# Second scores in the common PSUM banks for the first group, and gate/up products placed by half blocks for the second, in a cross-attention + soft-MoE kernel

## Chip, core and metric

One core of a Trainium2 chip. The time is the device time of one execution in microseconds; three runs of the kernel before gave 1177.79 to 1178.29, median 1177.96. Everything is float32. A profiled execution is one run with the hardware profiler on.

## What is computed

`x` is 16 sequences of 100 tokens by 256, `ctx` 16 contexts of 361 by 256. Cut to what matters:

```python
x = x + xattn(layernorm(x), ctx)      # 16 heads of 16: q@k.T/4, softmax over 361 keys, @v, @wo
x = x + ffn(layernorm(x))             # soft mixture of 16 experts with 64 slots each:
#   logits  = ln(x) @ slot_embeds.T             [tokens, 1024 slots]
#   slots   = softmax over experts(logits).T @ ln(x)
#   eout    = (gelu(slots@Wg + bg) * (slots@Wu + bu)) @ Wd + bd      per expert
#   out     = softmax over slots(logits) @ eout
```

## The kernel before

The batch is cut into groups of 2, 2, 4, 4, 4 sequences (`GROUPS`, L51). For each group there are three kinds of work: the **attention units** (`units`, L862), the **dispatch** of tokens to slots (`dispatch_quarter`, L927), and the **experts** (`experts`, L1264, with `down` L1231 and `combine_quarter` L1152). The experts of group g run while the attention of group g+1 is made, so only the first group's attention (the first 80 us or so) has no expert products beside it.

**A unit** is four heads of one sequence (`Unit`, L769), one per 32-row strip of the TensorE array, numbered here 0 to 7 in the first group (four for each of two sequences). Its steps:

- `maxima` (L781): first scores, four matmuls of 361 columns (L785) into the four banks of the fixed tile `at`; a VectorE reduction over them (L790) makes the row maxima.
- `queries` (L796): TensorE transposes the maxima (L799) into spare columns of `at` bank 0, VectorE adds them to the query (L801, tile `q`), which makes the second scores come out with the maximum subtracted.
- `exponentials` (L805): second scores, three blocks of keys by four strips, twelve matmuls of 100 columns (L810), into the same four banks of `at`; one ScalarE exponential over all of them (L818, `aT`).
- `values` (L824): twelve matmuls (L833) into a tile `cx` of the common pool; ScalarE copies it to `cxs` (L842).

Because first and second scores use the same `at`, a unit's first scores wait for the exponential of the unit before (`free_t`).

**PSUM** has eight banks: four for `at`, four for the common pool `ps_mm` (`mm_tile`, L169), which every other product takes in turn.

**Order.** Each engine runs its instructions in the order in which the program issued them. That order is made at build time by a planner: each stream of work is a Python generator that yields when it can go on (`when`), how many banks it needs and what it will use of TensorE, VectorE and ScalarE (`needs`); a model clock (`Clock`, L64) books a duration for every step. The loop at L1354 takes the first task that the model finds ready; in the first group the units lead, and other work (`fill`) is put between if it fits before the next step of the units. Where nothing fits, **warm products** are issued (`warm_up`, L1339: a matmul of the identity into bank 3 of `at`, which nothing reads). Fill work of the first group:

- `key_work` (L570) for sequences 0 to 3: transposed context `c_t` (L584), keys `k_ps` (L613) copied out by VectorE (L634) and ScalarE (L639), values `v_ps` (L673); a DMA by the SP queue writes the mask row into the keys (L653).
- `query_work` (L491), `out_work` (L701: reciprocal of the softmax sums, L713 and L714, a GpSimd multiply, `o_ps`, layernorm statistics, `xn_t`), `bo_work` (L413), `parameter_work` (L397).
- `slot_work` (L451): the layernorm of the slot embeddings: statistics on VectorE (L436, L437), scaling on ScalarE (L467), `se_t` (L476) and `seT` (L482).

In `experts`, the gate (`gp`) and up (`up`) products of one block (L1284, 8 matmuls of 128 columns in groups of two sequences) are issued without a break; the planner may put other work only between blocks.

Of the kernel before, what the change touches and what calls it, by code (L numbers as in the profile page):

```python
# [47 lines left out]
P = 128  # L48
# [7 lines left out]
SLACK = 0.6  # L56
BACKLOG = 2.5
ASIDE = ("out_work", "query_work", "key_work")
MASK_DMA = 5.0
COLD = 7.0  # L60
HOP = 0.12
# [68 lines left out]
def xattn_ffn_kernel(  # L130
# [38 lines left out]
    def mm_tile(name):  # L169
        return ps_mm.tile([P, 512], F32, tag="mm", name=name)  # L170
# [320 lines left out]
    def query_work(b, n=2):  # L491

        g = group_of[b]
        i0 = b - starts[g]
        yield x_t[g], 0, (0.0, 0.65 * n, 0.0)
        mv4 = two.tile([N, 2, 2], F32, tag="mv4", name="mv4")
        for i in range(n):
            ck.run("DVE", stats(accs[g][:, i0 + i, :], N, mv4[:, i, :]), x_t[g])
        r4 = rstd(mv4[:, :n, 1], N, n)
        t = ck.run("POOL", 0.7, ck.run("DVE", 0.15))  # L500
        yield t, 0, (0.0, 0.45 * n, 0.0)
        z4 = const.tile([N, 2, D], F32, tag="z4", name="z4")
# [12 lines left out]
        xT = const.tile([P, KD, 2 * N], F32, tag="xT", name="xT")  # L515
        ps = mm_tile("x_t")
        for kd in range(KD):
            for i in range(n):
                nc.tensor.transpose(
                    ps[:, (n * kd + i) * N : (n * kd + i + 1) * N],  # L520
                    z4[:, i, kd * P : (kd + 1) * P],
                    ident[:N, :N],
                )
# [12 lines left out]
        for oc in range(KD):  # L536
            for kd in range(KD):
                nc.tensor.matmul(  # L538
                    ps[:, oc * n * N : (oc + 1) * n * N],
                    lhsT=w_sb["wq"][:, kd, oc * P : (oc + 1) * P],  # L540
                    rhs=xT[:, kd, : n * N],
                    start=kd == 0,
                    stop=kd == KD - 1,
                )
        t = max(ck.pe(400 * n, t, ck.bank()), par_t[0] if par_t[0] < NEVER else 10.5)
        for oc in range(KD):
            src = ps[:, oc * n * N : (oc + 1) * n * N]
            nc.vector.tensor_scalar(
                qp[:, oc, 0, cols], src, hm[:, 0:1], qb[:, oc, 0:1], ALU.mult, ALU.add
            )  # L550
            nc.scalar.activation(
                qp[:, oc, 1, cols], src, AF.Identity, bias=qb[:, oc, 1:2], scale=hm[:, 1:2]
            )
            first = ck.psum_dve(100 * n, t)
            t = ck.copy(100 * n, first)
            if b == oc == 0:
                qps[b] = (qp, first)
        ck.free(t)
        for i in range(n):
            qps.setdefault(b + i, (qp, t))  # L560
        yield (lambda: bo_t[0]), 0, (0.0, 0.0, 0.0)
        a = accs[g][:, i0 : i0 + n, :]
        nc.gpsimd.tensor_tensor(a, a, bo_bc[:N].unsqueeze(1).to_broadcast([N, n, D]), ALU.add)
        t = ck.run("POOL", 0.55 * n)
        for i in range(n):
            with_bo[b + i] = t
# [202 lines left out]
    class Unit:  # L769
# [35 lines left out]
        def exponentials(self):  # L805
# [15 lines left out]
            if self.cb == 3:  # L821
                live.discard(self.b)

        def values(self):  # L824
            if self.cb == 0:
                live_cxs.add(self.b)
                cxs_of[self.b] = two.tile([P, 2, KD, N], F32, tag="cxs", name="cxs")
                fill.append(Task(out_work(self.b), ck, 2))
            cx = mm_tile("cx")
            for c in range(3):  # L830
                n = KC if c < 2 else S2 - 2 * KC
                for r in range(4):
                    nc.tensor.matmul(  # L833
                        cx[32 * r : 32 * r + 32, :N],
                        lhsT=values_of[self.b][
                            :n, c, 4 * self.oc + r, 2 * self.par : 2 * self.par + 2, :
                        ].rearrange("p k w -> p (k w)"),
                        rhs=self.aT[:n, r, c * N : (c + 1) * N],
                        start=c == 0,
                        stop=c == 2,  # L840
                    )
            nc.scalar.copy(cxs_of[self.b][:, self.par, self.oc, :], cx[:, :N])  # L842
            t = ck.copy(100, ck.run("PE", 0.72, self.t, values_t[self.b], ck.bank()))
            ck.free(t)
            cx_t[self.b, self.cb] = t

    free_t = [0.0]
    phase = [""]
    cx_t = {}
    group_of = {b: g for g, n in enumerate(GROUPS) for b in range(starts[g], starts[g] + n)}  # L850
# [6 lines left out]
    def values_ready(u):  # L857
        if u.b not in values_t or (u.cb == 0 and len(live_cxs) == 2):
            return NEVER
        return max(u.t, values_t[u.b])  # L860

    def units(g):  # L862
        last = None

# [6 lines left out]
                fill.append(Task(key_work(u.b + 2), ck))  # L871

        group = range(starts[g], starts[g] + GROUPS[g])
        for b in group:
            for cb in range(4):
                yield (
                    lambda: max(keys[b, cb][1], qps[b][1]) if (b, cb) in keys and b in qps else NEVER
                ), 0, (0.0, 0.0, 0.0)
                yield free_t[0], 0, (0.8, 1.7, 0.0)
                u = Unit(b, cb)  # L880
                u.maxima()
                if cb == 0 and b % 2 == 1 and b + 1 in group:
# [348 lines left out]
    def down(g, e, hts):  # L1231
# [29 lines left out]
            done_t[g, q] = t  # L1261
        give_back((k, "wd"), (k + 1, "wd"))

    def experts(g):  # L1264
        n = GROUPS[g]
        T = n * S
# [2 lines left out]
        for e in range(E):  # L1269
# [3 lines left out]
            for part in range(FC // FB):  # L1273
# [3 lines left out]
                for kind in range(2):  # L1277
                    yield (lambda: NEVER if slots_left[g, q] else slot_t[g, q]), 1
                    load_weights()
                    w = weights[k, ("wg", "wu")[kind]]  # L1280
                    ps = mm_tile(("gp", "up")[kind])
                    for f, fc in enumerate(fcs):
                        for kd in range(KD):
                            nc.tensor.matmul(  # L1284
                                ps[:, f * T : (f + 1) * T],
# [2 lines left out]
                                start=kd == 0,  # L1288
                                stop=kd == KD - 1,
                            )  # L1290
                    t = ck.pe(1024, slot_t[g, q], ck.bank())
                    for f, fc in enumerate(fcs):
                        cols = slice(f * T, (f + 1) * T)
                        if kind == 0:
# [59 lines left out]
    while streams["experts"]:  # L1354
# [29 lines left out]
        if waiting:  # L1384
            units_first = dispatches[:WINDOW] + units_first
            side = sorted(fill, key=lambda t: t.kind != "out_work")
            if group == 1 and 0 in qps:
                kinds = (
                    "early_work",
                    "bo_work",  # L1390
                    "query_work",
                    "parameter_work",
                    "slot_work",
                    "out_work",
                    "key_work",
                )
# [18 lines left out]
        if not begun:  # L1415
# [7 lines left out]
            else:  # L1423
                lead = [
                    i
                    for i, t in enumerate(tasks)
                    if t.kind in ("out_work", "all_experts") or t in dispatches[:1]
                ] if group > 1 else []
            soonest = min((ready[i] for i in lead), default=NEVER)
            by_keys = any(t.kind in ("key_work", "later_keys") and r <= now for t, r in zip(tasks, ready))  # L1430
            for i, t in enumerate(tasks):
# [6 lines left out]
                late = 0.15 + SLACK * pe  # L1438
                if not first_units:
                    fits = max(end, vector, scalar) <= soonest + late  # L1440
                elif phase[0] == "max":
                    fits = max(end, vector) <= soonest + late and scalar <= soonest + late + 1.2
                elif phase[0] != "queries":
# [10 lines left out]
            if ready[-1] <= now:  # L1454
                ready[:-1] = [NEVER] * (len(ready) - 1)
        first = next((i for i, r in enumerate(ready) if r <= now), None)
        if first is None:
            first = min(range(len(ready)), key=lambda i: ready[i])
            assert ready[first] < NEVER
            if not begun and now + 0.2 < ready[first] and phase[0] != "queries":  # L1460
                warm_up()
                continue
        task = tasks[first]
        begun = begun or task is streams["experts"]
        task.step()
        if task.done:
# [63 lines left out]
```

## Time and profile before

| | |
|---|---|
| median of three runs | 1177.96 us |
| profiled execution | 1179.8 us |
| its span | 1178.0 us |
| TensorE clock granted | 1.00 in every slice |
| VectorE, ScalarE, GpSimd busy | 632.8, 539.8, 150.9 us |
| warm products (L1337) | 53 matmuls, of which 9 before the first real product |

The page's first part gives each engine's busy time as a share of the span; its second part cuts the span into 40 slices of 29 us and gives the busy tenths of each. "Idle before" stands ahead of an instruction, with what released it. In float32 every matmul leaves two records in the trace (a transpose leaves one), so a row "x24" is twelve matmuls.

### The profile page before, as it was taken

What the parts mean: (1) busy time and instruction counts of PE and PEld (TensorE: products, weight loads), DVE (VectorE), ACT (ScalarE), POOL (GpSimd) and SP (SyncE); (2) the same over time, 40 slices, a digit from 0 to 9 for tenths busy, and PEclk for the clock granted to TensorE, in tenths of its full rate; (3) what the DMA queues carried; (4) which work ended last, traced back from release to release, by engine and by line L of the source; (5) the groups of instructions that cost most, each with busy time, mean ns of one, the idle gap of its engine ahead of it and who ended that gap; (6) DMA issues with size and microseconds to landing.
All of it is one profiled execution on the core that took longest, in us unless ns stands there. A gap on an engine that the chain in (4) does not pass through costs nothing.

```text
span 1178.0 us, 24309 instructions
## 1 busy us (share of the span) xinstructions
PE 1160.2 (98%) x9825; PEld 899.1 (76%) x9825; DVE 632.8 (54%) x1559; ACT 539.8 (46%) x1112; POOL 150.9 (13%) x255
## 2 busy tenths in 40 slices
PE   8899999999999999999999999999999999999998
PEld 6587778787787777767777776787878878777876
DVE  5755545565654565655386767656543455442222
ACT  3557554664544667434454634646312336314110
POOL 3110301013000131300010010304000003002000
PEclk9999999999999999999999999999999999999999
DMA  4412656543566603212341321333344343345431
GB/s 134 136 38 97 233 174 203 162 145 116 154 201 220 188 11 90 83 58 100 113 105 53 111 91 38 98 126 112 112 158 137 118 148 126 112 129 163 138 131 55
DMA packets 138588, 144.85 MB, mean 123 GB/s; under 512 B 45050, under 2 KB 97228, under 8 KB 138476
## 3 DMA queue, kind: packets, MB, share of 16 engines
q1 hardware_dynamic: 137258, 141.50, 38.6%
q8 instruction: 78, 1.28, 0.4%
q0 software_dynamic: 496, 1.12, 0.3%
q10 hardware_dynamic: 722, 0.67, 0.2%
q14 instruction: 34, 0.28, 0.1%
HBM read 141.60 MB, written 1.66 MB: 122 GB/s over the span
## 4 chain that ended last, share of the span: by engine, by line
PE 94%; DVE 2%; ACT 2%; DMA 1%; issue 1%; POOL 0%; SPq 0%; ACTq 0%; DVEq 0%; POOLq 0%
PE dn L1244 19%; PE gp L1284 19%; PE up L1284 19%; PE sl L1032 5%; PE po L1162 5%; PE at L810 4%; PE at L785 4%; PE lg L942 3%; PE cx L833 3%; PE v_ps L673 3%; PE k_ps L613 3%; PE at L1337 1%; PE o_ps L726 1%; DVE mxp L790 1%; DMA w_all<-in_L_ffn_Wd_dram 1%; PE q_ps L538 1%
## 5 line engine op out<-in xcount | busy, mean ns | idle before, releaser
L1284 PE MATMUL gp<-ring,w_all 128*128 128x256 f32 (+1 forms) x1280 | 247.8, 340 | 1.3 <-ACT lg_all L963 1.3
L1284 PE MATMUL up<-ring,w_all 128*128 128x256 f32 (+1 forms) x1280 | 246.6, 340 | 0.0
L1300 DVE SCALAR_TENSOR_TENSOR hT<-up,parT,ge 128x256 f32<-128x256 f32 (+1 forms) x320 | 119.6, 423 | 233.3 <-PE up L1284 163.0
L1244 PE MATMUL dn<-w_all,hT 128*64 128x256 f32 x2048 | 232.9, 382 | 1.4 <-DMA w_all<-in_L_ffn_Wd_dram 1.3
L1295 ACT ACTIVATE ge<-gp,parT 128x256 f32<-128x256 f32 (+1 forms) x320 | 116.8, 429 | 249.5 <-PE gp L1284 245.3
L1284 PEld LDWEIGHTS gp<-ring,w_all 128*128 128x128 f32 x1280 | 203.4, 191 | 27.5 <-issue 4.9
L1284 PEld LDWEIGHTS up<-ring,w_all 128*128 128x128 f32 x1280 | 203.7, 191 | 21.4 <-issue 1.2
L1244 PEld LDWEIGHTS dn<-w_all,hT 128*64 128x64 f32 x2048 | 142.7, 137 | 79.8 <-issue 8.3
L790 DVE TENSOR_REDUCE mxp<-at 100x4 f32<-100x1444 f32 x64 | 106.2, 1660 | 30.7 <-PE at L785 30.0
L1253 DVE TENSOR_TENSOR ring<-dn,bd_bc 128x512 f32<-128x512 f32 x64 | 44.2, 691 | 136.3 <-PE dn L1244 136.2
L818 ACT ACTIVATE aT<-at 121x1200 f32<-121x1200 f32 x64 | 74.9, 1170 | 64.3 <-PE at L810 60.9
L1295 ACT ACT_TABLE_LOAD x60 | 77.0, 1283 | 26.7 <-PE gp L1284 24.3
L1012 DVE STREAM_TRANSPOSE disp<-d_ex 32x128 f32<-32x128 f32 x256 | 77.4, 302 | 4.5
L717 POOL TENSOR_TENSOR cxs<-cxs,rs 128x100 f32<-128x100 f32 x63 | 24.8, 396 | 390.7 <-DVE rs L714 363.3
L1047 ACT ACTIVATE ring<-sl,parT 128x256 f32<-128x256 f32 x64 | 32.6, 561 | 67.9 <-PE sl L1032 67.9
L1032 PE MATMUL sl<-disp,xn 100*128 100x256 f32 x256 | 63.4, 388 | 0.2 <-ACT disp L1025 0.2
L1162 PE MATMUL po<-ring,lg_all 128*100 128x256 f32 x256 | 60.5, 383 | 0.4 <-DVE ring L1253 0.2
L997 POOL TENSOR_TENSOR d_ex<-d_ex,d_sm 128x400 f32<-128x400 f32 x28 | 23.8, 852 | 267.7 <-DVE d_sm L994 240.6
L810 PEld LDWEIGHTS at<-q,kT 32*121 32x121 f32 x1344 | 40.6, 180 | 19.9 <-issue 8.8
L1032 PEld LDWEIGHTS sl<-disp,xn 100*128 100x128 f32 x256 | 46.4, 190 | 10.3 <-issue 2.6
L810 PE MATMUL at<-q,kT 32*121 32x100 f32 x1344 | 49.9, 277 | 3.4 <-DVE q L801 3.3
L818 ACT ACT_TABLE_LOAD x36 | 46.2, 1283 | 14.2 <-PE at L810 6.2
(152 smaller groups left out, 1268.4 us busy)
## 6 DMA issues: line engine op xcount, KB each, us to landing
w_all<-in_L_ffn_Wg_dram SPq DMA_DIRECT2D x80, 512.0 KB
w_all<-in_L_ffn_Wu_dram SPq DMA_DIRECT2D x80, 512.0 KB
w_all<-in_L_ffn_Wd_dram SPq DMA_DIRECT2D x80, 512.0 KB
bd_bc<-in_L_ffn_bd_dram SPq DMA_DIRECT2D x80, 64.0 KB
c_sb<-in_ctx_dram SPq DMA_DIRECT2D x96, 44.0 KB
acc<-in_x_dram SPq DMA_DIRECT2D x7, 200.0 KB
out_dram<-acc SPq DMA_DIRECT2D x7, 200.0 KB
ring<-n_L_ffn_slot_embeds_dram POOLq DMA_DIRECT2D x1, 1024.0 KB, 6.6
```

Source lines behind the costliest of these rows:

```text
L785: nc.tensor.matmul(self.at[:N, r, :S2], lhsT=self.q[rows], rhs=self.k[rows], start=True, stop=True)
L790: nc.vector.tensor_reduce(mxv[:, :, m : m + 1], self.at[:N, :, :S2], AX.X, ALU.max, negate=True)
L810: nc.tensor.matmul(self.at[: KC + 1, r, c * N : (c + 1) * N], lhsT=self.k[rows, c * KC : c * KC + KC + 1], rhs=self.q2[rows], start=True, ...
L818: nc.scalar.activation(self.aT[: KC + 1], self.at[: KC + 1, :, : 3 * N], AF.Exp)
L1012: nc.vector.transpose(dst[toks, :, :, a, :], src[32 * a : 32 * a + 32, :, :, toks])
L1032: nc.tensor.matmul(sl[:, kd * 256 : (kd + 1) * 256], lhsT=xns[g][:, b0 + i, kd * P : (kd + 1) * P], rhs=disp[:, i, :], start=True, stop=True,)
L1162: nc.tensor.matmul(pos[i][:N, :D], lhsT=lg_all[:, slot, 2 * c + i, :], rhs=eouts_of(g, q)[:, c, 2 * p + i, :], start=c == 0, stop=c == 1,)
L1244: nc.tensor.matmul(dn[S * x : S * x + S, i * D : (i + 1) * D], lhsT=hts[x][fc // FB][0].rearrange("p (f b s) -> p f b s", f=FB, s=S)[:, fc ...
L1253: nc.vector.tensor_tensor(eouts_of(g, q)[:, j // 2, 2 * half : 2 * half + 2, :], dn.rearrange("p (b d) -> p b d", d=D), biases[k // 2].uns ...
L1284: nc.tensor.matmul(ps[:, f * T : (f + 1) * T], lhsT=w[:, kd, fc * P : (fc + 1) * P], rhs=slots_of(g, q)[:, j, kd].rearrange("p b s -> p (b ...
L1295: nc.scalar.activation(ge[:, cols], ps[:, cols], AF.Gelu, bias=col(8, e, fc))
L1300: nc.vector.scalar_tensor_tensor(out=hT[:, cols], in0=ps[:, cols], scalar=col(NPAR, e, fc), in1=ge[:, cols], op0=ALU.add, op1=ALU.mult,)
```

## The change

In the first group, `first_units` takes the place of the loop in `units`. The second scores no longer go to `at`: `half_exponentials` makes them in two halves of two strips each, six matmuls and two ScalarE exponentials of 300 columns per half, in four tiles of the common pool. So the next unit's first scores may be issued before the exponentials of this unit. The order asked for is: the maxima's transpose of unit n, first scores of n+1, products `cx` of n-1, both halves of n. Around it the planner's rules change: side work of the first group is let in by a budget per unit (`spare`), a task that needs VectorE alone may go first when VectorE is about idle (`IDLE`), and the order of preference of the side work is another. For group 1 (`HALVED`), the gate and up products of a block are issued as two halves of four matmuls with a yield between them. The model's time for a query copy is also changed.

```diff
+SPARE = 0.7
+IDLE = 0.15
@@ query_work
-        t = max(ck.pe(400 * n, t, ck.bank()), par_t[0] if par_t[0] < NEVER else 10.5)
+        tm = max(ck.pe(400 * n, t, ck.bank()), par_t[0] if par_t[0] < NEVER else 10.5)
...
-            first = ck.psum_dve(100 * n, t)
-            t = ck.copy(100 * n, first)
+            first = ck.psum_dve(100 * n, tm)
+            t = max(first, ck.copy(100 * n, tm))
@@ class Unit
+        def half_exponentials(self, half):
+            if half == 0:
+                self.aT = two.tile([P, 4, 3 * N], F32, tag="aT", name="aT")
+                self.parts = []
+            ps = [mm_tile(f"sc{r}") for r in range(2)]
+            t = max(ck.bank(), ck.bank())
+            for c in range(3):
+                for r in range(2):
+                    rows = slice(32 * (2 * half + r), 32 * (2 * half + r) + 32)
+                    nc.tensor.matmul(
+                        ps[r][: KC + 1, c * N : (c + 1) * N],
+                        lhsT=self.k[rows, c * KC : c * KC + KC + 1],
+                        rhs=self.q2[rows],
+                        start=True,
+                        stop=True,
+                    )
+            tp = ck.run("PE", 0.55, self.t, t)
+            for r in range(2):
+                nc.scalar.activation(
+                    self.aT[: KC + 1, 2 * half + r], ps[r][: KC + 1, : 3 * N], AF.Exp
+                )
+                t = ck.act("exp", 290, tp)
+                ck.free(t)
...
+    def first_units(finish, group):
+        held = before = None
+        nexts = [(b, cb) for b in group for cb in range(4)] + [None, None]
...
+        for n in nexts:
+            if held:
+                yield held.t, 0, (0.15, 0.25, 0.0)
+                held.queries()
+                phase[0] = "max"
+            if n and there(n):
+                yield from scores(n)
+            if before:
+                lt = before
+                yield (lambda: values_ready(lt)), 1, (0.7, 0.0, 0.3)
+                finish(before)
+                before = None
+            if held:
+                for half in range(2):
+                    yield held.t, 2, (0.5, 0.0, 0.9)
+                    held.half_exponentials(half)
+                before = held
...
@@ units
+        if g == 0:
+            yield from first_units(finish, group)
+            return
@@ experts
+    HALVED = (1,)
...
+                    bank = ck.bank()
                     for f, fc in enumerate(fcs):
+                        if g in HALVED and 2 * f == FB:
+                            ck.pe(512, slot_t[g, q], bank)
+                            yield 0.0, 0
...
-                    t = ck.pe(1024, slot_t[g, q], ck.bank())
+                    t = ck.pe(512 if g in HALVED else 1024, slot_t[g, q], bank)
@@ main loop: order of preference of the first group's side work
+                    "key_work",
+                    "query_work",
+                    "bo_work",
+                    "parameter_work",
+                    "out_work",
+                    "slot_work",
                     "early_work",
-                    "bo_work",
-                    "query_work",
-                    "parameter_work",
-                    "slot_work",
-                    "out_work",
-                    "key_work",
...
+                elif t.kind in ("slot_work", "out_work", "bo_work", "parameter_work"):
+                    fits = ready[i] <= now and max(pe, dve, act) <= spare[0]
...
+        if not begun and ck.t["DVE"] <= now + IDLE:
+            for i, t in enumerate(tasks):
+                alone = t.needs[0] == 0 and t.needs[1] > 0
+                if alone and t.kind in ("slot_work", "out_work") and t.ready() <= now:
+                    first = i
+                    break
```

More of the change, by code (lines that the diff above doesn't have):

```diff
@@ L822, in exponentials @@
                 live.discard(self.b)
+        def half_exponentials(self, half):
[21 more added lines that the diff above has]
+                ck.free(t)
+            self.parts.append(t)
+            if half == 1:
+                self.t = t
+                if self.cb == 3:
+                    live.discard(self.b)
         def values(self):
@@ L847, in xattn_ffn_kernel @@
     free_t = [0.0]
+    spare = [0.0]
     phase = [""]
@@ L860, in values_ready, with there, scores @@
         return max(u.t, values_t[u.b])
+    def first_units(finish, group):
+        held = before = None
+        nexts = [(b, cb) for b in group for cb in range(4)] + [None, None]
+        def there(n):
+            b, cb = n
+            return (b, cb) in keys and b in qps
+        def scores(n):
+            b, cb = n
+            yield (
+                lambda: max(keys[b, cb][1], qps[b][1]) if there(n) else NEVER
+            ), 0, (0.0, 0.0, 0.0)
+            yield free_t[0], 0, (0.8, 1.7, 0.0)
+            u = Unit(b, cb)
+            u.maxima()
+            free_t[0] = u.t
+            spare[0] = SPARE
+            made.append(u)
+        made = []
+        for n in nexts:
[15 more added lines that the diff above has]
+                before = held
+            if n and not made:
+                if before:
+                    lt = before
+                    yield (lambda: values_ready(lt)), 1, (0.7, 0.0, 0.3)
+                    finish(before)
+                    before = None
+                yield from scores(n)
+            held = made.pop() if made else None
     def units(g):
@@ L1426, in xattn_ffn_kernel @@
                     for i, t in enumerate(tasks)
-                    if t.kind in ("out_work", "all_experts") or t in dispatches[:1]
+                    if t.kind in ("out_work", "slot_work", "all_experts") or t in dispatches[:1]
                 ] if group > 1 else []
@@ L1463, in xattn_ffn_kernel @@
         task = tasks[first]
+        if task.kind in ("slot_work", "out_work", "bo_work", "parameter_work"):
+            spare[0] -= max(task.needs)
         begun = begun or task is streams["experts"]
```

## The prediction

> **What bounds the kernel now.** I read the page's shares and chain first, then the stretches of time, then TensorE's timeline, because the first tells which engine is short and the last where it stands still.
>
> ```profile
> PE 1160.2 (98%) x9825; PEld 899.1 (76%) x9825; DVE 632.8 (54%) x1559; ACT 539.8 (46%) x1112; POOL 150.9 (13%) x255
> ...
> PE 94%; DVE 2%; ACT 2%; DMA 1%; issue 1%; POOL 0%; SPq 0%; ACTq 0%; DVEq 0%; POOLq 0%
> ```
>
> TensorE is busy 98% and carries 94% of the chain. So the time is a sum: TensorE's useful work, its warm products, its idle time. A change that only moves work between its stages gains nothing; it must shrink idle or warm time, or else it pays for whatever it adds to the useful work. Idle is 17.8 us (1178.0 - 1160.2): 1.37 before the first product, 3.9 after the last, 1.34 at 89-90 us, some 4.8 in scattered gaps from 230 to 605 us, and 6.3 in the first group's attention, here unit 1:
>
> ```profile
> 19.00 0.39 PE L519 MATMUL x_t<-ident,z 100*128 100x100 f32 x2
> 20.27 1.16 PE L1337 MATMUL at<-ident 128*128 128x128 f32 x8 [0.88 <-DVE mxp L790]
> 21.27 0.25 PE L799 MATMUL at<-ident,mxp 100*128 100x100 f32 x1
> 21.87 0.89 PE L810 MATMUL at<-q,kT 32*121 32x100 f32 x24 [0.35 <-DVE q L801]
> 22.69 1.14 PE L538 MATMUL q_ps<-xT,wq 128*128 128x100 f32 x8
> ```
>
> Three things are to be seen. The four warm products (x8) did not fill the wait for the maxima: they waited 0.88 us for it, since their target bank was being read, and then cost 1.0 us more. The step from transpose to second scores costs 0.6 us (21.27 to 21.87), 0.35 of it idle, in every unit. Second scores, twelve matmuls, take 0.82 us (21.87 to 22.69).
>
> VectorE sets the other half of a unit:
>
> ```profile
> 54.60 0.26 DVE L801 TENSOR_TENSOR q<-at,qp 128x100 f32<-128x100 f32 x1 [0.67 <-PE at L799]
> ...
> 54.79 0.27 DVE L713 STREAM_SHUFFLE rs<-cxs 128x100 f32<-128x100 f32 x1
> ...
> 55.09 0.78 DVE L714 RECIPROCAL rs<-rs 128x100 f32<-128x100 f32 x1
> ```
>
> A shuffle and a reciprocal hold VectorE for 1.0 us (54.79 to 55.79, where the next begins). If they stand ahead of an addition `q`, it is late by that.
>
> **The account before, up to the first gate product (82.17 us).** Start 5.6 (1.37 idle, 4.21 for nine cold warm products), idle 6.3, the other 44 warm products 10.8 (their rows, about 0.24 each), useful work 59.5.
>
> **The change part by part.**
>
> *Second scores by halves: more TensorE work.* In the trace's records the 24 passes of one unit start in six rounds of four strips: 6.6 ns between strips, 106 ns between rounds, 184 ns after the first. A round takes as long with two strips as with four, because a strip waits for its own stream. A half has six rounds of two, so both have twelve. [...] But in the rows products start in the program's order and a waiting one is not overtaken, so only the last round of one half and the first of the next overlap: eleven rounds. [...] I take 0.53, **4.2 us** over eight units, ends 0 and 5.1.
>
> *Two exponentials of 300 columns per half* in place of one of 1200 (1.17 us, L818): the nearest row is the 361-column copy (0.46 us), so 4 x 0.4 to 0.46, about 0.6 us more on ScalarE per unit. ScalarE is busy 19.7 of the 39 us from 11 to 50, so this is hidden beside TensorE; uncovered it would be 5 us.
>
> *The exponential's wait goes; what is late next?* In the changed listing (order and semaphores, no times) first scores of n+1 still wait for `q` of n. So the 0.35 does not go: the transpose is followed by first scores instead of second, again 0.66 after it (14.38 to 15.04 for unit 0), or 0.54 idle, the transpose taking 0.12 and nothing standing between. And in units 2 and 6 a shuffle and reciprocal stand ahead of `q`.
>
> *Warm products.* The listing has 53 before the first gate product, as before: no gain. Eight stand right behind unit 4's first scores, three behind its second scores, two in unit 1, one behind unit 7's first scores; all wait for a reduction. Five more behind unit 7's transpose wait for `q`, which is queued behind the slot statistics' GpSimd power (1.68 us, L447) and its user on VectorE.
>
> *Walk.* I went down the changed listing with spacings from the trace: first scores 0.80, reduction ending 2.66 after their start, `cx` 0.66, both halves 1.35, two `v_ps` 0.96, two `k_ps` 1.41, `c_t` 0.73, `q_ps` 0.95, warm 0.23 each. Unit 0 starts at 11.73 as before.
>
> - Units 1 to 3: first scores at 16.6, 20.5, 24.4 (before: 17.55, 25.00, 31.26). The pipeline works: 3.9 us per unit. Here is the part that should gain.
> - But the second sequence's keys and values are still to be made (2.8 + 2.9), with `q_ps`, `c_t` and two `cx`: unit 4 at 38.2 (before 37.66). Its reduction ends at 41.2; TensorE idles 2.2 for it, then the eight warm products take 1.85.
> - Units 5, 6, 7 at 43.8, 47.8, 51.8 (before 44.36, 51.27, 57.66). One warm product after unit 7's first scores holds `cx` back by 1.9; the five before the last-but-one `cx` wait 1.1 and take 1.15.
> - The last `cx` ends at 63.1; before 64.47. But before had by then also made `bo_ps` 0.97, `se_t` 1.84, one `k_ps` pair 1.41, six `v_ps` 2.9, `o_ps` 0.86 and `c_t` 0.73: 8.7 us of work. So the changed kernel stands 8.7 - 1.4 = **7.3 us behind**.
> - The rest to the first gate product, item by item from the listing, is 19.2 of products plus 0.6 waiting: 82.9 (before 82.17), with two `k_ps` pairs and six `v_ps` (5.7) still undone: 0.7 + 5.7 = **6.4 behind**.
>
> The MASK rows and weights: the SP queue has the same DMAs in the same order; the mask rows of the second sequence are issued before the weights in both, so I cost this at nothing; if a row came late, first scores of unit 4 would wait for it.
>
> *After the first gate product.* Before, TensorE stood 1.34 us for ScalarE (softmax exponentials, two table loads of 1.28, gelu). The listing now has `k_ps` 1.41 where an up block (1.79) stood, and the second pair of `k_ps` waits for the same ScalarE copy: 1.7 of idle, then 0.5 waiting for the dispatch copy. That is **+0.9**, ends -1 and +3.
>
> *Group 1 by halves.* The same matmuls with the same weights; only the planner's choices move. TensorE's gaps there and where group 2 takes over (361 to 430 us: 0.36, 0.92, 0.21, 1.05, 0.19, 0.27, 0.62) are 3.6 us, all that can be gained there; the 0.36 and 0.92 are a weight DMA. In the listing attention units now run closer together there, more load on VectorE at once, which can open as much. I take 0, ends -3 and +3. The query copy's model time and the order of preference act only through the listing already walked.
>
> Sum: 6.4 + 0.9 = 7.3, of which I keep **6.5**, since rounding in a walk of sixty steps that always waits for the later of two times errs to the long side. The profiled execution took 1179.8 with a span of 1178.0, and would take about 1186.3; the median of the unprofiled runs, 1177.96, is 1.8 below it, and carries over: **1184.5 us**.
>
> **Rivals.**
>
> [...]
>
> *The banks of `at` are free when TensorE comes.* The one mechanism for a faster kernel: if each product before a wait runs later than in my walk, reductions and `q` are done when first scores and warm products come. My walk has waits in units 0 to 7 of 2.0 (`q` behind a shuffle and reciprocal, twice), 1.6 (`q` alone, three times), 5.0 (warm for a reduction: 0.3, 2.2, 0.6, 1.9) and 1.1 (warm for `q`): 9.7 us. Gone, the time is 1184.5 - 9.7 = 1174.8. It decides once 8.9 of the 9.7 are gone. For: three units at 3.9 us show how little is left to wait for. Against: the 0.88 above, which exactly this kind of warm product waited before.
>
> *Group 1's gaps close.* The finer blocks fill the 3.6 us and the dispatch stage too, and the delayed keys land in the 89 us gap: 6.5 - 5 leaves 1179.5, no change. Against: the gaps are waits for DMA, VectorE and GpSimd, not for a block to end.
>
> **How the numbers follow.** A measurement of this kernel can tell 0.2%, 2.4 us, from no change. Loss in the first group as walked: 0.60, at 1180.5 to 1190. Halves side by side: 0.13, about half of it within 0.2%, half slower. Banks free: 0.14, faster in four of five. Gaps close: 0.13, half within 0.2%, the rest to both sides. So faster 0.13, same 0.15, slower 0.72. The range for 8 in 10: the low end, 1175.5, takes in the rivals without change and leaves out the faster one; the high end adds the upper ends of the halves (0.9), the dispatch (2) and half of group 1 (1.5) and some for waits that I missed: 1190.5.
>
> **What would show it.** Right: second scores of a unit in about 1.35 us against 0.82; idle marked with `q` ahead of the first scores (L787 in the new file); warm products after unit 4's first scores preceded by about 2 us waiting for `mxp`; the first gate product near 83 us with keys of sequence 3 still unmade; TensorE's busy time some 4 us up. Wrong: the first gate product before 78 us, second scores in 0.9 us, or a TensorE without gaps from 360 to 430 us.

## The result, and the profile after

The changed kernel takes 1191.9 us (four runs, 1191.12 to 1194.48) against 1178.12 beside it: ratio 1.0122, 95% interval 1.0109 to 1.0135. It is 13.8 us slower; the prediction said 1184.5, with 1190.5 as the upper end. The profiled execution took 1191.56 us, its span 1189.7. The page's shares of the engines, its clock row and its chain:

```profile
PE 1168.2 (98%) x9825; PEld 908.5 (76%) x9825; DVE 631.3 (53%) x1560; ACT 548.6 (46%) x1141; POOL 151.1 (13%) x255
...
PEclk9889999999999999999999999999999999999999
...
PE 94%; DVE 3%; DMA 1%; ACT 1%; issue 0%; SPq 0%; ACTq 0%; POOL 0%; DVEq 0%; POOLq 0%
```

TensorE is busy 8.0 us longer and idle 3.7 us longer (21.5 against 17.8). The 8 in the second and third place of the clock row is new; before, the row was

```profile
PEclk9999999999999999999999999999999999999999
```

TensorE's timeline shows where (start, duration, records, idle ahead):

```profile
37.12 0.87 PE L787 MATMUL at<-kT,qp 32*100 32x361 f32 x8
40.20 2.05 PE L1430 MATMUL at<-ident 128*128 128x128 f32 x16 [2.21 <-DVE mxp L792]
...
45.38 0.94 PE L1430 MATMUL at<-ident 128*128 128x128 f32 x6 [0.87 <-DVE mxp L792]
...
46.76 0.87 PE L787 MATMUL at<-kT,qp 32*100 32x361 f32 x8 [0.35 <-DVE q L803]
47.55 0.72 PE L865 MATMUL cx<-aT,vpad 120*32 120x100 f32 x24
48.21 1.30 PE L836 MATMUL sc<-q,kT 32*121 32x100 f32 x24
49.44 0.30 PE L801 MATMUL at<-ident,mxp 100*128 100x100 f32 x1
50.52 0.87 PE L787 MATMUL at<-kT,qp 32*100 32x361 f32 x8 [0.78 <-DVE q L803]
53.18 0.80 PE L1430 MATMUL at<-ident 128*128 128x128 f32 x2 [1.79 <-DVE mxp L792]
53.90 1.23 PE L865 MATMUL cx<-aT,vpad 120*32 120x100 f32 x24
55.06 2.07 PE L836 MATMUL sc<-q,kT 32*121 32x100 f32 x24
57.06 0.43 PE L801 MATMUL at<-ident,mxp 100*128 100x100 f32 x1
57.85 2.50 PE L1430 MATMUL at<-ident 128*128 128x128 f32 x10 [0.35 <-DVE q L803]
```

Read it in two steps. First, the waits stand where the walk had them: for `mxp` 2.21 ahead of unit 4's eight warm products, 0.87 ahead of unit 5's three and 1.79 ahead of the one behind unit 7's first scores (walk: 2.2, 0.6, 1.9). Those for `q` are shorter, 0.35 and 0.78 where the walk had about 0.5 and 1.0. Second, from unit 7's warm product on every product takes longer: `cx` 1.23 instead of 0.72, second scores 2.07 instead of 1.30. The granted clock was 0.50 there. The stretches of time around it (start and end, length, busy time and records per engine, then the granted clock):

```profile
49.49:52.90 3.41, 1.12 (x10) 0.35 (x9) 2.39 (x4) 1.04 (x4) 0.40 (x1) 1.00 0.02 5
...
52.90:66.55 13.65, 12.99 (x121) 9.76 (x125) 3.63 (x15) 3.20 (x10) 2.77 (x3) 0.50 0.00 1
```

In the stretches shown here and below half clock lasted 3.41, 3.42, 6.82, 6.83, 13.65 or 23.89 us, each time one, two, four or seven steps of 3.41; here it is four. Where the clock changes several times in a run, all the changes lie on one grid of such steps (41.28, 44.70, 48.11, 51.52, 58.35 and 65.17 us in one below); from them I count the steps on at steady clock. In the step before the fall TensorE worked 1.12 us. Then it was busy nearly without a gap, 12.99 of 13.65 us. The records of the warm products start 213 ns apart in it (those from 57.85), and 112 ns apart at clock 1.00 (those from 40.20). So the halving costs up to 6.5 us here, by estimate: half of the 12.99. Before, the same stretch ran at full clock:

```profile
52.00:67.00 15.00, 13.95 (x184) 10.21 (x181) 12.02 (x32) 7.22 (x14) 2.12 (x5) 1.00 0.26 56
```

The first gate product comes at 86.46 us, 4.3 later than before (82.17); the wait for ScalarE behind it is there as walked:

```profile
86.46 1.95 PE L1377 MATMUL gp<-ring,w_all 128*128 128x128 f32 x16
...
92.17 0.60 PE L1106 MATMUL d_t<-ident,d_ex 128*100 128x128 f32 x4
94.68 1.48 PE L615 MATMUL k_ps<-cT,wk 128*128 128x361 f32 x4 [1.91 <-ACT lg_all L1049]
96.09 0.87 PE L787 MATMUL at<-ring,qp 32*100 32x361 f32 x8
97.34 0.92 PE L1118 MATMUL sl<-disp,xn 100*128 100x256 f32 x3 [0.39 <-ACT disp L1111]
```

From the first gate product to the end it is 1103.2 us against 1095.8, 7.4 more. Most of it is the late keys and values: in the trace two pairs of `k_ps` (from 90.96 and 94.68) and six `v_ps` (from 103.83 and 107.58) come behind it, some 5.5 us of work; before, none did.

### The profile page after: what moved, and what is told of

Its sections match the earlier page's. It is cut to its first block, busy times and chain, and to the rows that moved or that the text cites. A ratio compares the mean times of both kernels' runs of the same rounds, so it can differ in the third digit from the quotient of the medians.

```text
span 1189.7 us, 24325 instructions
## 1 busy us (share of the span) xinstructions
PE 1168.2 (98%) x9825; PEld 908.5 (76%) x9825; DVE 631.3 (53%) x1560; ACT 548.6 (46%) x1141; POOL 151.1 (13%) x255
## 3 DMA queue, kind: packets, MB, share of 16 engines
q8 instruction: 78, 1.28, 0.5%
q0 software_dynamic: 496, 1.12, 0.3%
## 4 chain that ended last, share of the span: by engine, by line
PE 94%; DVE 3%; DMA 1%; ACT 1%; issue 0%; SPq 0%; ACTq 0%; POOL 0%; DVEq 0%; POOLq 0%
PE dn L1330 19%; PE gp L1377 19%; PE up L1377 19%; PE sl L1118 5%; PE po L1248 5%; PE at L787 4%; PE at L812 4%; PE cx L865 3%; PE lg L1028 3%; PE v_ps L675 3%; PE k_ps L615 3%; PE at L1430 1%; PE o_ps L728 1%; DVE mxp L792 1%; PE q_ps L540 1%; PE at L801 1%
## 5 line engine op out<-in xcount | busy, mean ns | idle before, releaser
L1377 PEld LDWEIGHTS up<-ring,w_all 128*128 128x128 f32 x1280 | 204.8, 191 | 21.5 <-issue 1.1
L820 ACT ACTIVATE aT<-at 121x1200 f32<-121x1200 f32 x56 | 65.6, 1171 | 35.5 <-PE at L812 34.5
L874 ACT COPY cxs<-cx 128x100 f32<-128x100 f32 x64 | 15.5, 242 | 83.5 <-PE cx L865 81.2
L787 PE MATMUL at<-kT,qp 32*100 32x361 f32 x448 | 48.5, 502 | 4.2 <-DVE q L803 2.3
```

The source lines that it names most:

```text
L787: nc.tensor.matmul(self.at[:N, r, :S2], lhsT=self.q[rows], rhs=self.k[rows], start=True, stop=True)
L820: nc.scalar.activation(self.aT[: KC + 1], self.at[: KC + 1, :, : 3 * N], AF.Exp)
L1377: nc.tensor.matmul(ps[:, f * T : (f + 1) * T], lhsT=w[:, kd, fc * P : (fc + 1) * P], rhs=slots_of(g, q)[:, j, kd].rearrange("p b s -> p (b ...
```

## The experiments

The theory: the part of the loss that the prediction does not have is the halved clock, set off by waits of TensorE; the rest is the walk. Rivals: the half blocks cost something, the halves of the second scores cost much more than walked, or the order is itself worse.

**Half blocks alone**: the kernel before with `HALVED = (1,)` and the yield between the two halves of a block.

```diff
+                        if g in HALVED and 2 * f == FB:
+                            ck.pe(512, slot_t[g, q], bank)
+                            yield 0.0, 0
```

> The kernel before with the second group's gate and up products placed by halves, and nothing else. Theory (the loss lies in the first group: second scores and waits there some 7 us, and about 6 us because TensorE's clock is halved from 52.9 to 66.6 us): within 1.5 us of the kernel before, 1178, clock 1.000. Rival (the half blocks cost time, since attention units crowd together where the third group takes over): 1181 to 1184.

Measured 1177.13 us, ratio 0.9992 (0.9985 to 0.9999), clock 1.000, as expected. The half blocks cost nothing.

**The first group's change alone**: `HALVED = ()` in the changed kernel.

> The changed kernel without the halves of the second group. Theory: 1190 to 1193.5, and the clock falls at 52.9 us again, as the first 112 us are the same. Rival (half blocks cost): 1186 to 1188.

Measured 1194.03 us, 1.0141 (1.0118 to 1.0164), half a microsecond above the expected range. The loss is in the first group. The clock fell, but not where I expected. Stretches of this run:

```profile
37.87:41.28 3.41, 1.20 (x12) 0.45 (x11) 2.87 (x7) 1.58 (x4) 0.00 (x0) 1.00 0.86 261
...
41.28:44.70 3.42, 3.42 (x17) 3.38 (x17) 0.34 (x2) 0.00 (x0) 0.00 (x0) 0.50 1.02 359
44.70:48.11 3.41, 2.14 (x35) 1.59 (x34) 2.12 (x3) 1.26 (x4) 0.00 (x0) 1.00 1.09 280
48.11:51.52 3.41, 3.06 (x18) 1.65 (x18) 0.58 (x3) 0.10 (x1) 0.00 (x0) 0.50 0.22 61
51.52:58.35 6.83, 4.27 (x89) 2.98 (x87) 5.09 (x9) 1.61 (x6) 0.84 (x2) 1.00 0.01 2
58.35:65.17 6.82, 6.46 (x67) 5.53 (x70) 2.53 (x10) 1.83 (x6) 2.33 (x3) 0.50 0.00 0
```

TensorE's order in this stage is that of the changed kernel, yet the clock falls three times: after unit 4's wait (1.20 busy of 3.41), after a step with 2.14, and behind unit 7's waits (1.62 busy of 3.41). The halved time is 13.65 us in all again. The grid lies otherwise against the program here. Unit 4's wait of 2.21 us (38.95 to 41.16) falls into a single step of it (37.87 to 41.28); in the changed kernel's own run the same wait (37.99 to 40.20) was cut in two by a step's end at 39.25 (52.90 - 13.65), and the clock held: the step from there to 42.66 was busy 2.14 us, as long as the one at 44.70 here, behind which it fell. So I take it that which wait sets it off hangs in part on where the grid lies, which no run shows by itself. That the grid differs from run to run is shown: a step ends 0.12 us behind this wait here, and 0.95 us before its end there.

**One warm product less**: the one behind unit 7's first scores is left out.

> The changed kernel without the one warm product behind unit 7's first scores, which waited 1.8 us for the reduction and held the products cx back. Theory (the clock falls when TensorE worked too little within one window of 3.41 us, here 49.5 to 52.9, where it was busy 1.2 us): that window now holds a cx and second scores, so the clock does not fall at 52.9; but the next wait, for q behind the slot statistics, moves up into the window 52.9 to 56.3 with some 3 us of idle, so the clock falls at 56.3 instead; time 1188 to 1193. Rival (it falls at 52.9 whatever stands in that one wait, because products on 32 rows count for little over a longer time): clock again 0.5 from 52.9. Second rival (the fall has to do with the 1.8 us stretch alone): no fall at all, 1184.

Measured 1189.95 us, 1.0095 (1.0078 to 1.0112), in the expected time but not by the expected way: the grid was again the other one, and the clock fell at 41.29 and 48.12, one step each. The wait for `q`, behind which the theory put a new fall, is there and lasts 2.54 us. TensorE was busy for half of the step that holds most of it, and the clock held:

```profile
58.35:61.77 3.42, 1.75 (x30) 1.63 (x34) 2.07 (x8) 0.00 (x0) 1.64 (x2) 1.00 0.00 0
```

So neither the theory nor its rivals are shown. A single wait can't be judged in one profile.

**Feeding TensorE through its waits**: in the units, warm products go to common banks, where they need not wait for the reduction; six more lie in unit 7's wait and ten more in the following one for `q`.

```diff
-        warm_product()
+        n_warm[0] += 1
+        if streams["units"] and phase[0]:
+            for _ in range(7 if n_warm[0] == 26 else 3 if 27 <= n_warm[0] <= 31 else 1):
+                nc.tensor.matmul(mm_tile("warm")[:, :P], lhsT=ident, rhs=ident, start=True, stop=True)
+        else:
+            warm_product()
```

> The changed kernel with the warm products of the units put into common banks, where they need not wait for the reduction, and six more of them in unit 7's wait and ten more in the wait for its q. Theory: the clock stays at 1.0 (about 6 us won), the warm products now lie inside the waits (1.8 + 0.7 + 1.8 us won at units 4, 5 and 7): 1181 to 1184. Rival (the clock falls because of the first group's 32-row products, not of the waits): clock below 1, 1187 to 1189.

Measured 1187.7 us, 1.0077 (1.0058 to 1.0096): 4.2 us less, with sixteen matmuls more. The units keep full clock, but it now falls behind the dispatch wait:

```profile
87.42:90.84 3.42, 1.51 (x6) 0.68 (x4) 0.99 (x3) 2.85 (x12) 0.00 (x0) 1.00 0.00 0
90.84:97.67 6.83, 6.83 (x25) 4.91 (x25) 4.84 (x10) 3.31 (x7) 0.00 (x0) 0.50 0.26 80
```

So the time missed the expectation and lies in the rival's range, but the rival's cause does not fit, since the units ran at full clock in the profiled run. What the clock is worth can be read from the four runs of this one kernel: with mean clocks of 1.000, 0.998, 0.997 and 0.996 they took 1185.05, 1186.45, 1188.94 and 1189.87 us. By estimate, a mean of 0.996 over 1188 us stands for 9.5 us at half clock, worth up to 4.8; the last of these runs is 4.8 above the first. The next run, with eight warm products in the dispatch wait too:

```diff
+                if (g, p, q) == (0, 0, 1):
+                    for _ in range(8):
+                        warm_product()
```

> The kernel of the run before with fed waits, and eight more warm products in the wait of the dispatch (89 us there), on the free bank 3. Theory (a window of 3.41 us in which TensorE is busy less than about half halves the clock of the next): no window before the end falls below a half, clock 1.000 all through, the 6.8 us at half clock are gone: 1183.5 to 1185. Rival (warm products count for little, or the wait itself costs the time): clock below 1 again, 1187 to 1188.

No run shows half busy, as in that theory, to be a limit: with the first group's change alone the clock had fallen behind a step with 2.14 us of work in 3.41. Measured 1186.71 us, 1.0062 (1.0047 to 1.0077), between both expectations; the intervals of this kernel and the one before it overlap. The cores view of the profiled run shows that the clock stayed at full until the program's end:

```profile
core 0: 1185.4 us, clock 1.000
```

Its profiled execution, 1187.18 us, is 0.9 above the 1186.3 that the walk gave for one, although 24 warm products were added. That is near the walk but no test of it, since this kernel also has its own warm products in common banks, inside waits that the walk counts in full.

**The wait for `q` taken away too**: the transpose of the maxima in a common bank, so that the next first scores need not wait until `q` has been read out of `at`.

```diff
-            tp = self.at[:, 0, 512 - N :]
+            tp = (mm_tile("tp") if self.b < GROUPS[0] else self.at[:, 0, 412:])[:, :N]
```

> As the run before it, and the transpose of the maxima of the first group in a common bank, so that the next first scores need not wait for q. Theory: the idle ahead of first scores goes (0.35 three times, 0.78 twice, 2.6 us in all): 1181 to 1182.5. Rival (first scores that come earlier wait elsewhere, for the reduction or for mask rows): within 1 us of the run before it.

Measured 1184.16 us, 1.0044 (1.003 to 1.0058), clock 1.000. The time is above the expected range, which started from a faster run; the difference to the run before it is the expected one (2.55 for 2.6), though the intervals of the two overlap. The trace agrees: no first scores of the units wait for `q` any more, here units 2 and 3,

```profile
20.20 0.87 PE L787 MATMUL at<-kT,qp 32*100 32x361 f32 x8
...
23.27 0.87 PE L787 MATMUL at<-kT,qp 32*100 32x361 f32 x8
```

and from unit 0's first scores to the first gate product it is 67.3 us instead of 69.3.

**The halves measured alone**: the kernel before, with the first group's second scores issued strips 0 and 1 first, then 2 and 3; same banks, one exponential.

```diff
-            for c in range(3):
-                for r in range(4):
+            halves = ((0, 1), (2, 3)) if self.b < GROUPS[0] else ((0, 1, 2, 3),)
+            for c, r in [(c, r) for h in halves for c in range(3) for r in h]:
```

> The kernel before, and in the first group the twelve second scores issued strips 0 and 1 first, then strips 2 and 3, into the same banks and with one exponential: the price of the halves by itself. Theory (a round of two strips takes what a round of four takes): second scores 1.24 us instead of 0.82, 0.42 for each of eight units, all of it on the path, since the exponential waits for them: 1181 to 1182. Rival (different strips run side by side): 1178.

Measured 1182.27 us, 1.0031 (1.0024 to 1.0038). Unit 1, whose row was 0.89 before:

```profile
22.68 1.18 PE L810 MATMUL at<-q,kT 32*121 32x100 f32 x24 [0.35 <-DVE q L801]
23.79 1.14 PE L538 MATMUL q_ps<-xT,wq 128*128 128x100 f32 x8
```

The next product starts 1.11 us after the first score here, 0.82 before: 0.29 a unit. In the changed kernel it is 1.23 (48.21 to 49.44), 0.41 a unit.

The starts of the single records say how the halves overlap. Here, counted from the first score, two strips have their rounds at 0, 184, 290, 396, 502 and 608 ns, and between them lie the starts of the other two, at 303, 487, 593, 698, 804 and 910: the second half begins when the first has done three of its six rounds, 0.29 us later than side by side. (Which record belongs to which strip is read from the spacing; it is not marked.) In the changed kernel one strip of the second half begins at 302, the other only at 432, in units 1, 2 and 5. That is the other 0.12. Why this strip is late was not tested.

Eight times 0.29 are 2.3 of the 3.9 us here. The rest goes with one step of halved clock (31.02 to 34.43), by estimate worth up to 1.7; the four of the twenty runs with mean clock 1.000 took 1180.17 to 1181.46, 1.8 to 3.1 above the kernel before.

**The warm products' bank alone**: half blocks and the common banks for warm products on the kernel before, with its order of units.

```diff
+        if streams["units"] and phase[0]:
+            nc.tensor.matmul(mm_tile("warm")[:, :P], lhsT=ident, rhs=ident, start=True, stop=True)
+        else:
+            warm_product()
```

> The kernel before with the second group's half blocks and with its warm products of the first group in common banks, where they do not wait for the maxima or the exponential. Theory: the four, three and four warm products that came 0.88, 0.72 and 0.88 us late now lie inside those waits, 2.4 us won: 1174 to 1175.5. Rival (a wait that they held up ends elsewhere, at the maxima, which come when they come; then only what ran past the maxima is won): 1176 to 1177.

Measured **1174.19 us, 0.9957 (0.9943 to 0.9972)**: faster than both kernels. TensorE's timeline, unit 1:

```profile
19.68 0.39 PE L519 MATMUL x_t<-ident,z 100*128 100x100 f32 x2
19.91 1.08 PE L1348 MATMUL warm<-ident 128*128 128x128 f32 x8
20.95 0.31 PE L799 MATMUL at<-ident,mxp 100*128 100x100 f32 x1
21.61 0.89 PE L810 MATMUL at<-q,kT 32*121 32x100 f32 x24 [0.35 <-DVE q L801]
```

The same four warm products now lie inside the wait, instead of 0.88 us of waiting and then 1.0 us of work. From unit 0's first scores to the first gate product it is 67.2 us, against 70.4 in the run with half blocks alone. That is the 3 us between the two kernels.

**The same bank and the free transpose in the changed kernel**, without the 24 extra products:

> The changed kernel with its own warm products in common banks and the transposes in a common bank, without the extra products of the fed runs (24 fewer). Theory: the extra products stood in waits, so leaving them out wins little, and TensorE falls under about half busy in a window at unit 7, at its q or in the dispatch, so the clock is halved in one window or more: 1184 to 1187, clock 0.995 to 0.999. Rival (the extra products were mostly cost, 24 of 0.23 us): 1179 to 1181, clock 1.000.

Measured 1181.8 us, 1.0036 (1.0023 to 1.0049): between both expectations. The profiled run fell to half clock for two steps; the one run with clock 1.000 took 1180.34. Against the kernel before with its warm products in common banks (1174.19), the new order is some 6 us slower even in this single run, although its transposes are freed besides. Its median is 2.4 us below that of the kernel with the 24 extra products, so these did not earn more than they cost; the intervals of the two overlap, so that they lost is not shown.

**No warm products in the first group**, neither in the changed kernel nor in the one before; the fourteen ahead of the first unit stay.

```diff
-        warm_product()
+        if not (streams["units"] and phase[0]):
+            warm_product()
```

> The changed kernel with none of the warm products from the first unit to the first gate product. Theory: about 9 us of products go, but the waits behind them stay and more windows fall under half busy, so the clock is at a half in more windows than in the changed kernel (over 14 us in all): 1188 to 1198, clock below 0.994. Rival (warm products are only cost, the clock does not depend on them): 1183 to 1186, clock 0.994.

Measured 1187.11 us, 1.0075 (1.006 to 1.009), clock 0.988 in the profiled run:

```profile
36.14:39.56 3.42, 1.24 (x13) 0.48 (x11) 2.88 (x7) 1.58 (x4) 0.00 (x0) 1.00 0.98 320
39.56:63.45 23.89, 22.64 (x226) 15.26 (x227) 12.57 (x31) 7.26 (x22) 3.17 (x4) 0.50 0.30 92
```

Seven steps of halved clock follow unit 4's wait, and still it is 4.8 us faster than with the warm products, between both expectations: in the changed kernel these cost more than the clock that they hold. Here less comes of the clock than in the run with fed waits: the two runs with a mean of 0.988 took 1188.46 and 1187.51, the two with 0.993 took 1186.71 and 1185.21.

> The kernel before with none of the warm products from the first unit to the first gate product. Theory: as above, the clock, at 1.000 before, now falls in one to three windows, which takes back what the products cost: 1175 to 1183, clock 0.995 to 0.999. Rival (only cost): 1168 to 1173, clock 1.000.

Measured 1178.48 us, 0.9998 (0.9989 to 1.0006), clock 0.995, as expected: there they pay for themselves. That they do so through the clock is what the single runs suggest: the one with a mean of 0.999 took 1175.12, those with 0.995 took 1178.6 to 1178.8.

**`cx` behind the transpose**, in the fastest kernel: the products `cx` of the first group are placed between transpose and second scores, to fill the 0.35 for `q`.

```diff
-                if last:
+                if last and g:
...
+                if last and not g:
+                    lt = last
+                    yield (lambda: values_ready(lt)), 1, (0.7, 0.0, 0.3)
+                    finish(last)
```

> The kernel of the run with half blocks and warm products in common banks (1174.2), and in the first group the products cx of the unit before placed between a unit's transpose and its second scores, where TensorE waits 0.35 us for q. Theory: the idle ahead of second scores goes (eight times 0.35) and the time of cx is taken out of a stretch that warm products filled: 1171 to 1173. Rival (VectorE's reductions and copies are what a unit lasts, so more warm products take the place, 55 where there were 39): 1173.5 to 1176.

Measured 1185.16 us, 1.0059 (1.004 to 1.0078): 11 us slower than the kernel it was made from, both expectations missed. Its first gate product comes at 80.06 (79.65 without the edit); the loss lies later, where the planner's order has changed too. A stretch in group 1, then TensorE's timeline there:

```profile
228.00:246.00 18.00, 16.16 (x136) 11.56 (x136) 8.22 (x17) 8.91 (x27) 2.02 (x3) 0.81 0.28 93
```

```profile
231.99 0.72 PE L833 MATMUL cx<-aT,vpad 120*32 120x100 f32 x24
233.84 0.30 PE L799 MATMUL at<-ident,mxp 100*128 100x100 f32 x1 [1.13 <-DVE mxp L790]
234.86 0.64 PE L1024 MATMUL d_t<-ident,d_ex 128*100 128x128 f32 x4 [0.71 <-POOL d_ex L1001]
235.43 1.55 PE L810 MATMUL at<-q,kT 32*121 32x100 f32 x24
```

Two waits (1.13 and 0.71) and then second scores at 1.55 instead of 0.89: the clock fell here as well, for two steps. By estimate, half clock for 6.8 us costs at most 3.4. It leaves most of the 11 us to other gaps and work in the new order, which I did not trace one by one.

## Why the prediction was off

- **The direction held, and so did the walk of the units.** The first scores start at 10.94, 15.79, 19.60, 23.37, 37.12, 42.74, 46.76 and 50.52. The walk had 11.73, 16.6, 20.5, 24.4, 38.2, 43.8, 47.8, 51.8; the run began 0.8 earlier (its first `c_t` took 0.79 us instead of 1.41, the warm products around it 4.05 and 1.28 instead of 4.21 and 1.38), and less this the largest error is 0.5.
- **The step that failed** is the sum at the head of the prediction, "TensorE's useful work, its warm products, its idle time". It has no term for the clock. All spacings of the walk were taken from a trace at clock 1.00, so each wait was priced at its own length and the clock behind it at nothing, without a reason. "One warm product after unit 7's first scores holds `cx` back by 1.9" was right as a wait (1.79); but at its end the clock fell, and stayed at a half for 13.65 us, which by estimate costs up to 6.5. The row "1.00 in every slice" was taken over to an order of products that opens longer waits.
- **Size.** From unit 0's first scores to the first gate product the walk had 71.2 us (82.9 - 11.73) and the run 75.5 (86.46 - 10.94): 4.3 more. The waits in it were 1.5 shorter than walked (8.2 instead of 9.7) and the halves about 1 shorter, so the clock's part is some 6 to 7 by this sum, an estimate that agrees with the 6.5. Against the forecast for the profiled execution, 1186.3, the run took 1191.56, 5.3 more: 3.6 up to the first gate product (the 4.3, less the 0.8 of the earlier start), 0.8 behind it (7.4 where the walk had 5.7 + 0.9), and the 0.8 that I had taken off the walk for rounding.
- The **other 2.1** of the miss is the step from profiled execution to median: before, the median was 1.7 below it; after, it is 0.3 above. The 1.8 did not carry over. The time of the changed kernel moves with the clock of the run: three of the four had a mean of 0.994 and took 1191.1 to 1192.2, the one with 0.992 took 1194.48.
- **Second scores by halves**: 0.53 a unit forecast, as five more rounds of 0.106, with 0 and 0.64 (six more) as the ends. No run shows any of the three: measured are 0.29 with this split in the old banks, and in the changed kernel 0.41 in units 1, 2 and 5, about 0.2 in units 0 and 4 (their rows last 1.08 and 1.11 us instead of 0.89) and 0.8 in unit 3, where a warm product stands between the halves; units 6 and 7 ran at half clock. Some 3 us in all, by estimate, for 4.2. A round of two strips does take what one of four takes (with the split in the old banks it starts at 0, 184, 290, 396, 502 and 608 ns, four strips before at 0, 185, 290, 396, 502 and 608); why it does was not tested. The step "a waiting one is not overtaken", from which the eleven rounds came, does not fit the records: the halves overlap by three rounds and not by one. That 0.53 came near the measured 0.41 is in part luck, since a strip that starts late (432 ns instead of 302) made up for a part of it.
- **Exponentials of 300** took 1.36 us a unit (four of 0.42, overlapping) for 1.17 and were hidden, as forecast: TensorE waits for one only once in the first group, 0.20 us. **The dispatch stall**: 1.91 + 0.39 = 2.3, where the walk had 1.7 + 0.5.
- **Group 1**: half blocks at 0, shown by the run with them alone. The rival that its gaps close fell: TensorE still waits 0.52, 0.71, 0.61 and 1.55 us between 220 and 430 us.
- **The rival of free banks** had the right lever and the wrong premise. I asked whether `at` would happen to be free; the runs show what it is worth to make it free: warm products and the transpose in common banks take the changed kernel from 1191.9 to 1181.8. Part of that is the clock (means of 0.997 to 1.000 instead of 0.992 to 0.994). But the kernel before gains from the first of these as well, and with it ends at 1174.19. The new order of units itself brought no gain in any run.

Shown by runs: the half blocks are free, the warm products' bank is worth 3 us, and with fed waits the time of one kernel grew from 1185.05 to 1189.87 us as its mean clock fell from 1.000 to 0.996. Shown by the traces: the walked waits, the late keys and values, and the half clock behind unit 7's wait. Not shown one by one is how the 13.8 us divide, since no run has the changed order at full clock and nothing else changed. Runs at full clock with other edits lie 2 us (the single run at 1180.34, with both banks freed) to 8 us (1186.71, with 24 more products) above the kernel before. With the warm products' bank freed in both, the new order is some 6 us behind. So it would lose without the fall of the clock too, as the prediction said; how much exactly is not shown.

## What to carry to other kernels

A filler that waits for the same thing as the work behind it fills nothing: here four warm products waited 0.88 us and then took 1.0 more, and with such products in common banks, inside the wait, the kernel took 1174.19 us instead of 1177.13. So give a filler a bank of its own. Price a wait on the busiest engine twice, by its length and by the clock behind it (here 1.79 us, and then 13.65 us at half clock), and look for stretches in which a change leaves the engine mostly idle, as in the 3.41 us with 1.12 of work here. In a kernel ordered by a planner an edit in one stage is also an edit in every later one: walk or measure those too.

## What the hardware showed that was not expected

- The clock fell behind steps of 3.41 us in which TensorE was busy 1.12, 1.20, 1.24 and 1.51 us, but also behind 2.14 (the first group's change alone) and 2.39 (both banks freed). It held behind 1.75 (one warm product less) and behind 2.07 (the kernel before). The busy time of a step alone does not decide; what else counts stays open.

```profile
49.16:52.57 3.41, 2.39 (x26) 1.84 (x20) 1.52 (x9) 1.36 (x4) 1.68 (x1) 1.00 0.00 0
52.57:59.39 6.82, 6.79 (x71) 4.50 (x73) 2.05 (x7) 1.60 (x5) 1.10 (x2) 0.50 0.01 2
...
88.71:92.12 3.41, 2.07 (x19) 1.82 (x17) 1.33 (x5) 2.86 (x12) 0.00 (x0) 1.00 0.43 154
```

- It stayed low for one step (41.28 to 44.70), two, four (52.90 to 66.55) or seven (39.56 to 63.45), although TensorE was busy 12.99 of 13.65 and 22.64 of 23.89 us in the long ones. Why was not found.
- Two halves in different strips and banks neither ran side by side nor one after the other: second scores took 1.23 us instead of 0.82 in units 1, 2 and 5 of the changed kernel, and 1.11 with the same split in the old banks, where the second half began 0.30 us after the first.
